# Setup weights in small tiles and a new model of engines and transfers in the planner of a four-layer graph network

## The chip, the cores and the metric

The kernel runs on one core of a Trainium2 chip. The core has five engines with a queue each: TensorE (PE in the profile; its weight loads are shown as PEld), VectorE (DVE), ScalarE (ACT), GpSimd (POOL) and SyncE (SP), which issues most of the transfers. Each engine works through its own queue in order. The metric is the device time of one execution in microseconds (us); lower is better. Before the change it is 3286.79 us, the median of three runs (3286.14 to 3287.27).

## The reference

The input is 64 graphs of 256 nodes with 256 features each (x), and a 256 x 256 integer adjacency of zeros and ones per graph. Four layers follow one another, each on a normalised and rectified copy of x, and each is added to x:

```
h = relu(layernorm(x)); x = x + GAT(h, adj)      # layer 0: 4 heads of 64, slope 0.2, elu
h = relu(layernorm(x)); x = x + typed_GAT(h,adj) # layer 1: 4 heads of 64, slope 0.01,
                                                 #   bias, relu, + h, layernorm per head, gamma, beta
h = relu(layernorm(x)); x = x + GAT(h, adj)      # layer 2: 1 head of 256, slope 0.2
h = relu(layernorm(x))                           # layer 3: three rounds of
for i in range(3):                               #   m = h @ weight[i]
    h = GRU(adj^T @ (h @ weight[i]), h)          #   gates r, z, n from w_ih, w_hh
x = x + h
```

An attention layer projects h to Wh, scores node i against node j with leaky_relu(src_i + dst_j), where src and dst are products of Wh with fixed vectors, masks with the adjacency, takes the softmax over j and sums the rows of Wh with these weights. Everything is fp32.

## The kernel before

**Tiling.** Two graphs make a pair; there are 32 pairs (NP). For a pair, 512 node rows lie as 4 chunks (C) of 128 partitions. The work is written per pair in the functions layer0, layer1, layer2 and gru.

**Setup (group -1).** Weights are loaded once. For each attention layer the score vectors are folded into the weights: score_column multiplies a weight block with a broadcast vector (tensor_mul on VectorE, into a temporary of class g), reduces it, and copies the result into an extra column of w0e, w1e or w2e. There are 12 such products of 128 x 256. The graph convolution's weight[i] and the GRU's w_ih are multiplied once into wc (input_gates, L925), so that a round of the GRU needs adj^T h, then wc, and whh. For that, weight (w3) and w_ih (wih) are loaded into two tiles of class cb4_, one each. The norms of the score columns are checked (check_columns) and the GRU's biases are combined (gate_biases).

**A pair.** norm takes statistics on VectorE (L962, L963), a power on GpSimd (L971, L972) and applies them on ScalarE (L980). transposed turns the result on TensorE (L997). project multiplies with w0e, w1e or w2e (L1019), and ScalarE copies to wh. factors transposes one score column to a row (L1053), takes its exponential (L1060), sends the row to DRAM on ScalarE's queue (rd, L1065) and loads it back from there, broadcast to all partitions, on SyncE's queue into cb (L1066; 1 MB for a layer of 4 heads, class cb4_, of which there are two slots). weights makes the unnormalised attention pt on VectorE from cb and the other factor f (L1087, four instructions a head) and takes the minimum with cap, which holds the mask (L807). attend_head multiplies pt with wh on TensorE (L1107). gru runs three rounds; each has 12 groups of matmuls of 128x512 (gate, L1318: ht with whh, ag with wc), the aggregation with the adjacency (L1304) and transposes (L1332). layer0 also loads x (L1144) and the adjacency (at, L1146, one slot), takes degrees (L1156), casts the adjacency on GpSimd (am) and builds cap (L1164, L1177).

**The order.** Nothing above is issued in the order in which it is written. Each step becomes an operation with an engine, an estimated cost in ns and the buffers it reads and writes. Buffers belong to classes with a fixed number of slots (cb4_: 2, at: 1, g: 9, bank: 8). _Schedule.run first gives each operation a due time, backwards from the end of its pair, (p + 1) x 100000 ns: a successor's due time less 3 times its cost (STRETCH) less HOP. Then it plays the engines forward in a model: whenever an engine is free, it takes the operation with the earliest due time whose inputs are there and whose buffers have a free slot. The sequence that comes out is fixed as the order of each engine's queue on the chip. The model's times exist in this planning alone; on the chip the engines wait for one another through semaphores. In the model, an instruction's result is visible to another engine HOP = 300 ns after its cost, to its own engine at once; a transfer takes its bytes at DMA_RATE plus DMA_LATENCY, and SyncE may issue any number of them ahead.

Vector instructions that go through the helper vec are all shown as L807 in the profile; the tile names tell them apart.

Of the kernel before, what the change touches and what calls it, by code (L numbers as in the profile page):

```python
# [517 lines left out]
SLOPES = (0.2, 0.01, 0.2)  # L518

# [18 lines left out]
class _Schedule:  # L538
# [8 lines left out]
    HOP = 300  # L547
    DMA_LATENCY = 2000
    DMA_RATE = 250.0
    STRETCH = 3.0  # L550

# [67 lines left out]

    def run(self):  # L620
        ops = self.ops
        for o in reversed(ops):
            late = self.end[o.group]
            for s in o.succs:
                if s.group == o.group or o.group not in self.end or o.group < 0:
                    late = min(late, s.due - self.STRETCH * s.cost - self.HOP)
            if o.nbytes:
                late -= self.DMA_LATENCY + o.nbytes / self.DMA_RATE
            o.due = late
# [17 lines left out]
        while True:  # L647
            for e in engines:
                if not idle[e]:
                    continue  # L650
                held = []
                while able[e]:
# [6 lines left out]
                    if all(len(self.free[c]) >= n for c, n in need.items()):  # L659
# [9 lines left out]
                        post(clock + o.cost, "free", o)  # L669
# [7 lines left out]
            while events and events[0][0] == clock:  # L677
                _, _, kind, o = heapq.heappop(events)
                if kind == "free":
                    idle[o.engine] = True  # L680
                    t = clock
                    if o.nbytes:
                        self.dma_free = max(self.dma_free, clock) + o.nbytes / self.DMA_RATE
                        t = self.dma_free + self.DMA_LATENCY
                        post(t, "done", o)
                    else:
                        post(t + self.HOP, "done", o)
                        for s in o.succs:
                            if s.engine == o.engine:
                                s.waits -= 1  # L690
                                if s.waits == 0:
                                    heapq.heappush(able[s.engine], (s.due, s.index))
                elif kind == "done":
                    done += 1
                    for s in o.succs:
                        if o.nbytes or s.engine != o.engine:
                            s.waits -= 1
                            if s.waits == 0:
                                heapq.heappush(able[s.engine], (s.due, s.index))
# [9 lines left out]
def _fast_path(  # L709
# [38 lines left out]
    P = 128  # L748
# [66 lines left out]
    def dma(engine, nbytes, emit, reads=(), writes=(), takes=()):  # L815
        op(engine, 450 if engine == "sp" else 120, emit, reads, writes, takes, nbytes)
# [4 lines left out]
    w3, wih = buf("cb4_", [P, L, DC, D]), buf("cb4_", [P, DC, G])  # L821
# [33 lines left out]
    for i in range(L):  # L855
        dma("sp", 1 << 18, lambda i=i: nc.sync.dma_start(
            w3.tile[:, i], w3t[i].rearrange("(c p) d -> p c d", p=P)), (), [(w3, i)])
    dma("sp", 3 << 18, lambda: nc.sync.dma_start(
        wih.tile, wih_t.rearrange("(c p) g -> p c g", p=P)), (), [wih])
# [4 lines left out]
    def score_column(B_we, w_ap, vec_buf, v_ap, dst, k, dc, s):  # L864
# [3 lines left out]
        vec(nc.vector.tensor_mul, 330, view, w_ap, v_ap,  # L868
            reads=[(B_we, (dc, "w")), vec_buf], writes=[tmp])
        col = lambda: cols.tile[:, dc, k : k + heads]  # L870
        vec(nc.vector.tensor_reduce, 330, col, view, AX.X, OP.add, reads=[tmp], writes=[(cols, (dc, k))])
        vec(nc.vector.tensor_copy, 80, dst, col, reads=[(cols, (dc, k))], writes=[(B_we, (dc, s))])
# [47 lines left out]
    def input_gates(i, dc, g0, g1):  # L920
        ps = bank()

        def mm():
            for ec in range(DC):
                nc.tensor.matmul(  # L925
                    ps.tile[:, : g1 - g0],
                    lhsT=w3.tile[:, i, ec, dc * P : (dc + 1) * P],
                    rhs=wih.tile[:, ec, g0:g1],
# [4 lines left out]
        op("pe", (g1 - g0) * 3.4, mm, [(w3, i), wih], [ps])  # L933
        vec(nc.scalar.copy, 150 + (g1 - g0), wc[:, i, dc, g0:g1], lambda: ps.tile[:, : g1 - g0],
            reads=[ps], writes=[(B_wc, (i, dc, g0))], engine="act")

    for i in range(L):
        for dc in range(DC):
            for g0 in (0, 512):
                input_gates(i, dc, g0, min(g0 + 512, G))  # L940
# [8 lines left out]
    op("dve", 300, gate_biases, [bi, bh], [B_bg])  # L949
# [5 lines left out]
    def norm(xt, cls):  # L955
# [19 lines left out]
        vec(nc.vector.scalar_tensor_tensor, 120, lambda: mv.tile[:, 3, :], lambda: mv.tile[:, 0, :], -1.0,  # L975
# [13 lines left out]
    def transposed(xn, cls):  # L989
        ht = buf(cls, [P, DC, S])  # L990

        def block(dc):
# [8 lines left out]
            op("pe", 470, emit, [xn], [ps], takes=[ht])  # L1001
# [7 lines left out]
    def project(ht, we, B_we, heads, width, shift):  # L1009
# [4 lines left out]
        def rows(c):  # L1014
# [12 lines left out]
            op("pe", 910, emit, [ht, B_we], [ps], takes=[wh])  # L1027
# [440 lines left out]
```

## Time and profile before

| | |
|---|---|
| median of the runs | 3286.79 us |
| profiled execution: time, span | 3288.5 us, 3286.6 us |
| mean granted TensorE clock | 0.989 |
| PE busy in 0 to 100, 100 to 200, 200 to 300 us | 60.0, 59.2, 99.8 us |
| PE busy in 3200 to 3287 us | 74.2 us |
| DVE, ACT, POOL busy over the span | 2368.8, 1453.9, 1103.6 us |
| first GRU matmul (L1318) | 170.8 us |
| granted TensorE clock at 120 to 130 us | 0.50 |

The span runs from the first to the last instruction; the rest of an execution's time lies around it. A line of a group reads: line, engine, operation, output tile <- input tiles, shapes, count, then what the engine waited for in brackets. In the chain of waits and in the waits view, "A <- B" means that A stood idle until B was done. For SyncE the queue itself is shown (SPq): its waits are spent by the queue in front of a transfer, with everything behind it.

### The profile page before, as it was taken

To read this page: it belongs to the slowest core of one execution; us is meant where nothing else is said; L and a number is where in the kernel's file an instruction comes from. 1 tells how busy PE (TensorE), PEld (TensorE's weight loads), DVE (VectorE), ACT (ScalarE), POOL (GpSimd) and SP (SyncE) were. 2 spreads that over 40 slices of the span, in tenths; PEclk is the share of its full clock that TensorE was granted. 3 is DMA by queue.
4 is the path that set the end of the run, shared out by engine and by line. 5 is a ranking of instruction groups with operands and counts; after the bars stand their busy time and mean duration, and the time that the engine had idled before them with its cause. 6 is when DMAs were issued, how large, how long until landed. Compare 5 with 4: busy or idle time off the path is not lost.

```text
span 3286.6 us, 49515 instructions
## 1 busy us (share of the span) xinstructions
PE 3184.5 (97%) x19094; PEld 1890.3 (58%) x19094; DVE 2368.8 (72%) x4977; ACT 1453.9 (44%) x2829; POOL 1103.6 (34%) x1096
## 2 busy tenths in 40 slices
PE   6499999999999999999999999999999999999998
PEld 4355555655565565565555555655565565565554
DVE  6947777777777777777777777777777777776752
ACT  4244444544444444444544444544444444444432
POOL 2423332343432334332424432343432334332330
PEclk8799999999999999999999999999999999999999
DMA  4101110111110111011101110111111111011000
GB/s 137 43 21 39 39 43 30 49 38 41 46 47 32 36 43 49 33 44 41 43 30 56 40 43 30 49 37 41 48 38 41 36 43 49 33 36 36 30 10 14
DMA packets 73012, 134.02 MB, mean 41 GB/s; under 512 B 7872, under 2 KB 59840, under 8 KB 64576
## 3 DMA queue, kind: packets, MB, share of 16 engines
q1 hardware_dynamic: 68688, 129.38, 11.3%
q8 instruction: 153, 2.51, 0.3%
q10 hardware_dynamic: 4080, 1.39, 0.2%
q14 instruction: 91, 0.75, 0.1%
HBM read 113.38 MB, written 17.37 MB: 40 GB/s over the span
## 4 chain that ended last, share of the span: by engine, by line
PE 87%; DVE 4%; POOL 4%; issue 1%; ACT 1%; DVEq 0%; POOLq 0%; ACTq 0%
PE bank L1318 56%; PE bank L1107 11%; PE bank L1019 9%; PE bank L1304 5%; PE bank L997 3%; PE bank L1332 2%; POOL mean L1240 1%; DVE o L807 1%; POOL g L807 1%; DVE g L807 1%; POOL o L807 1%; ACT g L807 0%; PE bank L1177 0%; PE bank L1053 0%; DVE hl L807 0%
## 5 line engine op out<-in xcount | busy, mean ns | idle before, releaser
L1318 PE MATMUL bank<-ag,wc 128*128 128x512 f32 x2304 | 1058.7, 597 | 0.0
L1318 PE MATMUL bank<-ht,whh 128*128 128x512 f32 x2304 | 1052.3, 594 | 0.0
L807 ACT ACTIVATE g<-bank,bg 128x512 f32<-128x512 f32 x576 | 395.3, 686 | 1001.3 <-PE bank L1318 995.5
L1318 PEld LDWEIGHTS bank<-ag,wc 128*128 128x128 f32 x2304 | 425.6, 190 | 493.0 <-issue 481.6
L1318 PEld LDWEIGHTS bank<-ht,whh 128*128 128x128 f32 x2304 | 421.0, 190 | 455.3 <-issue 442.6
L807 DVE SCALAR_TENSOR_TENSOR g<-g,g 128x512 f32<-128x512 f32 x384 | 285.7, 744 | 319.8 <-ACT g L807 316.4
L1087 DVE TENSOR_SCALAR pt<-cb,f 128x256 f32<-128x256 f32 x1152 | 399.5, 421 | 114.6 <-PE bank L1107 100.8
L807 POOL TENSOR_TENSOR g<-ht,g 128x512 f32<-128x512 f32 x192 | 321.0, 1688 | 418.3 <-ACT g L807 418.3
L1107 PE MATMUL bank<-wh,pt 128*64 128x65 f32 x9216 | 405.1, 244 | 48.7 <-DVE pt L807 48.4
L1107 PEld LDWEIGHTS bank<-wh,pt 128*64 128x64 f32 x9216 | 331.7, 140 | 186.3 <-issue 122.4
L807 DVE TENSOR_TENSOR pt<-pt,cap 128x1024 f32<-128x1024 f32 x288 | 373.6, 1327 | 3.3
L807 POOL TENSOR_TENSOR o<-o,bias_b 128x512 f32<-128x512 f32 x64 | 92.8, 1450 | 576.5 <-DVE o L807 363.8
L1304 PE MATMUL bank<-am_r,hl 128*128 128x256 f32 x1536 | 236.1, 301 | 5.8 <-DVE hl L807 5.4
L807 ACT ACTIVATE g<-g,bg 128x512 f32<-128x512 f32 x192 | 133.2, 716 | 228.7 <-DVE g L807 228.7
L980 ACT ACTIVATE xn<-xt,mv 128x256 f32<-128x256 f32 x384 | 205.2, 589 | 65.3 <-DVE mv L807 64.9
L971 POOL TENSOR_SCALAR mv<-mv 128x4 f32<-128x4 f32 x128 | 31.1, 243 | 595.3 <-DVE mv L963 553.2
L1304 PEld LDWEIGHTS bank<-am_r,hl 128*128 128x128 f32 x1536 | 196.8, 190 | 40.9 <-issue 24.6
L962 DVE BATCH_NORM_STATS2 st<-xt 128x6 f32<-128x256 f32 x512 | 208.2, 407 | 12.1 <-DMA xt<-in_x_dram 8.8
L807 ACT COPY ht<-bank 128x512 f32<-128x512 f32 x256 | 139.5, 590 | 120.3 <-PE bank L997 114.3
L807 DVE TENSOR_TENSOR g<-g,bank 128x512 f32<-128x512 f32 x192 | 127.6, 683 | 74.8 <-PE bank L1318 74.8
L807 DVE RECIPROCAL rs<-bank 128x4 f32<-128x4 f32 (+1 forms) x384 | 56.3, 164 | 162.4 <-PE bank L1107 162.2
L1034 ACT COPY wh<-bank 128x264 f32<-128x264 f32 (+1 forms) x256 | 96.2, 376 | 132.2 <-PE bank L1019 130.2
(91 smaller groups left out, 3522.4 us busy)
## 6 DMA issues: line engine op xcount, KB each, us to landing
cb<-rd SPq DMA_DIRECT2D x64, 1024.0 KB
xt<-in_x_dram SPq DMA_DIRECT2D x32, 512.0 KB
at<-in_adj_dram SPq DMA_DIRECT2D x32, 512.0 KB
out_dram<-xt SPq DMA_DIRECT2D x32, 512.0 KB
cb<-rd SPq DMA_DIRECT2D x32, 256.0 KB
rd<-row ACTq DMA_DIRECT2D x64, 8.0 KB
cb<-in_L_gnn_w_ih_dram SPq DMA_DIRECT2D x1, 768.0 KB
cb<-in_L_gnn_weight_dram SPq DMA_DIRECT2D x3, 256.0 KB
```

Of the source, the lines that this page charges most:

```text
L807: op(engine, cost, lambda: fn(*[a() if callable(a) else a for a in args], **kw), reads, writes)
L962: nc.vector.bn_stats(st.tile[:, c, :], xt.tile[:, c, :])
L980: op("act", 610, lambda: nc.scalar.activation(xn.tile[:, c, :], xt.tile[:, c, :], AF.Relu, bias=mv.tile[:, 3, c : c + 1], scale=mv.tile[:, ...
L997: nc.tensor.transpose(ps.tile[:, c * P : (c + 1) * P], xn.tile[:, c, dc * P : (dc + 1) * P], ident)
L1019: nc.tensor.matmul(ps.tile[:, : heads * W], lhsT=ht.tile[:, dc, c * P : (c + 1) * P], rhs=we[:, dc].rearrange("p h w -> p (h w)"), start=( ...
L1034: nc.scalar.copy(wh.tile[:, :, c, :], src)
L1087: nc.vector.tensor_scalar(pt.tile[:, b, jc, :].rearrange("p (i n) -> p i n", n=P), cb.tile[:, h, 2 * b : 2 * b + 2, :], f.tile[:, 1, h, c ...
L1107: nc.tensor.matmul(ps[q * Q : (q + 1) * Q], lhsT=pt.tile[:, b, jc, i0 : i0 + Q], rhs=wh.tile[:, h, 2 * b + jc, :w], start=(jc == 0), stop= ...
L1240: nc.gpsimd.tensor_tensor(var.tile, var.tile, nhalf[:, :R], op=OP.pow)
L1304: nc.tensor.matmul(ps.tile[:, b * N : (b + 1) * N], lhsT=hl.tile[:, k, 2 * b + sc, :], rhs=am.tile[:, 2 * b + sc, :], start=(k == 0 and sc ...
L1318: nc.tensor.matmul(ps.tile, lhsT=w[:, dc, g * P : (g + 1) * P], rhs=v.tile[:, dc, :], start=(first and dc == 0), stop=(last and dc == DC - 1),
L1332: nc.tensor.transpose(ps.tile[:, c * P : (c + 1) * P], ht.tile[:, j, c * P : (c + 1) * P], ident)
```

## The change

The diff has five parts.

1. w3 and wih are no longer two tiles of class cb4_ but six tiles of 128 x 2 x 256 of class g (three each), loaded with six transfers of 256 KB. input_gates runs over three blocks of 256 gate columns in place of blocks of 512 and 256.
2. The 12 products of score_column are issued on GpSimd in place of VectorE.
3. The planner holds SyncE back when more than DMA_AHEAD = 2000 ns of transfers are outstanding in its model. DMA_RATE becomes 220.
4. The planner's model of engines: HOP becomes a value per engine, an OVERLAP per engine frees an engine before its result is there, and a follower on the same engine, TensorE's apart, waits for the result and the hop too. Due times use MARGIN = 200 where they used HOP.
5. Estimated costs of many operations are changed, by a few per cent to some 20 per cent, up or down.

PACE names the 100000 that was written out before. The diff, cut:

```diff
+    OVERLAP = {"pe": 0, "act": 90, "dve": 80, "pool": 0, "sp": 0}
+    HOP = {"pe": 250, "act": 120, "dve": 120, "pool": 150, "sp": 0}
     DMA_LATENCY = 2000
-    DMA_RATE = 250.0
+    DMA_RATE = 220.0
+    DMA_AHEAD = 2000
     STRETCH = 3.0
+    MARGIN = 200.0
...
+    def enable(self, ops, able):
+        for o in ops:
+            o.waits -= 1
+            if o.waits == 0:
+                heapq.heappush(able[o.engine], (o.due, o.index))
...
-                    late = min(late, s.due - self.STRETCH * s.cost - self.HOP)
+                    late = min(late, s.due - self.STRETCH * s.cost - self.MARGIN)
...
+                if e == "sp" and self.dma_free > clock + self.DMA_AHEAD:
+                    continue
...
-                        post(clock + o.cost, "free", o)
+                        post(clock + o.cost - self.OVERLAP[e], "free", o)
...
-                        t = self.dma_free + self.DMA_LATENCY
-                        post(t, "done", o)
+                        post(self.dma_free + self.DMA_LATENCY, "done", o)
+                        post(max(clock, self.dma_free - self.DMA_AHEAD), "dma", o)
                     else:
-                        post(t + self.HOP, "done", o)
-                        for s in o.succs:
-                            if s.engine == o.engine:
...
+                        post(clock + self.OVERLAP[o.engine] + self.HOP[o.engine], "done", o)
+                    if o.engine == "pe":
+                        self.enable([s for s in o.succs if s.engine == "pe"], able)
                 elif kind == "done":
                     done += 1
-                    for s in o.succs:
-                        if o.nbytes or s.engine != o.engine:
...
+                    self.enable([s for s in o.succs if s.engine != "pe" or o.engine != "pe"], able)
...
-    w3, wih = buf("cb4_", [P, L, DC, D]), buf("cb4_", [P, DC, G])
+    w3, wih = ([buf("g", [P, DC, D]) for _ in range(3)] for _ in range(2))
...
-    dma("sp", 3 << 18, lambda: nc.sync.dma_start(
-        wih.tile, wih_t.rearrange("(c p) g -> p c g", p=P)), (), [wih])
+    for k in range(3):
+        dma("sp", 1 << 18, lambda k=k: nc.sync.dma_start(
+            wih[k].tile, wih_t.rearrange("(c p) g -> p c g", p=P)[:, :, k * D : (k + 1) * D]), (), [wih[k]])
...
-        vec(nc.vector.tensor_mul, 330, view, w_ap, v_ap,
-            reads=[(B_we, (dc, "w")), vec_buf], writes=[tmp])
+        vec(nc.gpsimd.tensor_tensor, 700, view, w_ap, v_ap, op=OP.mult,
+            reads=[(B_we, (dc, "w")), vec_buf], writes=[tmp], engine="pool")
...
-        op("pe", (g1 - g0) * 3.4, mm, [(w3, i), wih], [ps])
+        op("pe", 870, mm, [w3[i], wih[k]], [ps])
...
-            op("pe", 470, emit, [xn], [ps], takes=[ht])
+            op("pe", 445, emit, [xn], [ps], takes=[ht])
...
-            op("pe", 910, emit, [ht, B_we], [ps], takes=[wh])
+            op("pe", 895, emit, [ht, B_we], [ps], takes=[wh])
...
-        op("pe", 150, emit_t, [wh], [ps])
+        op("pe", 115, emit_t, [wh], [ps])
...
-                op("dve", 440, lambda b=b, jc=jc: emit(b, jc), [cb, f], [(pt, (b, jc))])
+                op("dve", 425, lambda b=b, jc=jc: emit(b, jc), [cb, f], [(pt, (b, jc))])
...
-        op("pe", 980, emit, [pt, wh], [ps], takes=[o])
+        op("pe", 1040, emit, [pt, wh], [ps], takes=[o])
...
-            op("pe", 250, emit, parts(cap_n, (2 * b, 2 * b + 1)), [(ps, b)], takes=[cap])
+            op("pe", 230, emit, parts(cap_n, (2 * b, 2 * b + 1)), [(ps, b)], takes=[cap])
...
-            op("pe", 880, lambda: attend(ps.tile[:, : D + 1], pt, wh, c, 0, D + 1), [pt, wh], [ps])
+            op("pe", 910, lambda: attend(ps.tile[:, : D + 1], pt, wh, c, 0, D + 1), [pt, wh], [ps])
...
-            op("pe", 920, emit, [hl, am], [ps], takes=[ag])
+            op("pe", 1060, emit, [hl, am], [ps], takes=[ag])
...
-            op("pe", 1740, emit, [v, B_w], [ps])
+            op("pe", 1725, emit, [v, B_w], [ps])
...
-                vec(nc.gpsimd.tensor_tensor, 1330, lambda: d.tile, lambda: ht.tile[:, j, :],
+                vec(nc.gpsimd.tensor_tensor, 1500, lambda: d.tile, lambda: ht.tile[:, j, :],
```

The other changed costs are of the same kind.

## The prediction

> **What bounds the kernel now.** I read the page's busy table and slices first, then the busy time by stretch of the first 175 us, then the waits of SyncE's DMA queue, then the timeline around the stretch where TensorE is idle.
>
> ```profile
> PE 3184.5 (97%) x19094; PEld 1890.3 (58%) x19094; DVE 2368.8 (72%) x4977; ACT 1453.9 (44%) x2829; POOL 1103.6 (34%) x1096
> PE   6499999999999999999999999999999999999998
> DVE  6947777777777777777777777777777777776752
> ```
>
> TensorE is the bound for all but the first two slices (82 us each) and the end. The rest, 3286.6 - 3184.5 = 102 us, is what can be won without doing less matmul work. The chain of waits shows how regular the middle is: the same piece comes back every three pairs.
>
> ```profile
> 1672.34 15.45 PE bank L1318 x36
> 1968.31 15.45 PE bank L1318 x36
> ```
>
> (1968.31 - 1672.34)/3 = 98.66 us per pair, which I call the period. In the middle TensorE waits for almost nothing; this is the waits view for 300 to 3100 us (total, times, longest, in us):
>
> ```profile
> PE bank L1304 <- DVE hl L807: 5.4, 9, 0.6
> PE bank L1332 <- DVE ht L807: 0.7, 1, 0.7
> ```
>
> So 6 us in 2800 is all that a better order can take from waits there. The start is different. Busy time by stretch (window, its length, then each engine):
>
> ```profile
> 0.00:16.60 16.60, 0.03 (x1) 0.03 (x1) 7.74 (x27) 3.73 (x6) 4.12 (x13) 1.00 0.68 197
> 16.60:30.00 13.40, 12.81 (x48) 8.75 (x49) 10.11 (x45) 8.15 (x19) 3.96 (x7) 1.00 0.85 277
> 30.00:49.80 19.80, 19.80 (x101) 15.14 (x100) 3.46 (x9) 14.91 (x33) 6.37 (x13) 1.00 0.28 97
> 49.80:110.00 60.20, 33.86 (x535) 29.01 (x533) 54.95 (x128) 15.61 (x37) 10.09 (x10) 0.77 0.20 75
> 110.00:167.00 57.00, 20.07 (x228) 15.81 (x228) 51.19 (x111) 12.66 (x26) 33.30 (x30) 0.68 0.07 24
> ```
>
> Columns after the length are PE, PEld, DVE, ACT, POOL. From 49.8 to 167 us VectorE is busy 106.1 of 117.2 us and TensorE only 53.9: there VectorE is the bound, because the GRU of pair 0, which feeds TensorE, can't start until pair 0 has passed three attention layers. From 30 to 49.8 us VectorE works 3.46 us and is idle 16.3. The timeline names why:
>
> ```profile
> 26.74 0.34 ACTq L1065 DMA_DIRECT2D rd<-row  x1
> 45.31 0.82 SPq L1066 DMA_DIRECT2D cb<-rd  x2
> 49.81 3.97 DVE L1087 TENSOR_SCALAR pt<-cb,f 128x256 f32<-128x256 f32 x12 [2.14 <-DMA cb<-rd]
> 170.84 2.42 PE L1318 MATMUL bank<-ht,whh 128*128 128x512 f32 x4
> ```
>
> The row goes out at 26.74, the broadcast load that brings it back is issued at 45.31, the first attention weights follow at 49.81, the first GRU matmul at 170.84. The queue's own waits say what it stood behind:
>
> ```profile
> SPq L1146 <- DVE rs L1156: 11.3, 1, 11.3
> SPq L1066 <- PE bank L925: 10.0, 1, 10.0
> SPq L1146 <- ACT cap_n L1150: 3.5, 1, 3.5
> ```
>
> First a load of the adjacency of pair 2 (L1146) waits for its one slot till 35.2; then the cb load waits 10.0 us for the input-gate products (L925), since w3 and wih sit in both cb4_ slots. Later, where nothing is in its way, the same step takes:
>
> ```profile
> 224.72 0.25 ACTq L1065 DMA_DIRECT2D rd<-row  x1
> 225.88 0.34 SPq L1066 DMA_DIRECT2D cb<-rd  x1
> 229.97 1.38 DVE L1087 TENSOR_SCALAR pt<-cb,f 128x256 f32<-128x256 f32 x4 [1.23 <-DMA cb<-rd]
> ```
>
> That is 1.2 us and 4.1 us, 5.3 in all, against 23.1 at the start.
>
> **What the Trainium skill says.** "DMA: Bandwidth & Descriptors", section on the anatomy of one DMA: a semaphore wait of a DMA is spent on the issuing sequencer before dispatch. The trace agrees: the two SP waits above hold everything queued after them. "SBUF — State Buffer", section "Who interferes with whom": VectorE and GpSimd share a port pair under an exclusive lock, also when a tensor_tensor reads two SBUF inputs. It fits: at 118.65 a GpSimd product of 128x512 takes 3.18 us and at 123.13 one takes 1.26, with VectorE active beside the first. "GPSIMD Engine Reference", section 3.1, prices tensor_tensor at 1.96 times VectorE.
>
> **The change part by part.** (1) Small tiles for w3 and wih: both cb4_ slots are free from the start, so the 10.0 us wait goes. (2) The other stall, pair 2's adjacency load ahead of it, goes only if the planner puts the cb load ahead in SP's order. The limit on outstanding transfers is in the planner alone and adds no wait on the chip; it only changes the order in SP's queue. With it, SP in the model holds back and picks by due time when there is room. In the model the row is back near 21 us: adding costs and hops from the load of x, through norm, transpose and projection. By then the model's rate of 220 bytes/ns allows 4.5 MB; what is more urgent (x and adjacency of pairs 0 and 1, w0, w1, vectors, w2) is 3.9 MB, and 2.25 MB of w3, wih and whh, which the present order already puts ahead of x of pair 2, are still mostly out. So I take the cb load to come before pair 2's adjacency. Then it is issued at 26.74 + 1.2 to 1.4 = 28.1 and lands with 4.1 to 4.5 (the same step at 45.31 took 4.5): VectorE starts at 32.2 to 32.6 in place of 49.81, a shift of 17.2 us. If the DMA queue is not drained by then (277 GB/s in 16.6 to 30), it is up to 1 MB / 277 GB/s = 4 us later.
>
> From there the stage is VectorE's, so the shift carries through to the first GRU matmul, less what is now free: the 3.46 us that VectorE does in 30 to 49.8 (degrees, checks) then fall into the busy stage. 17.2 - 3.5 = 13.7 us; if the 11.1 us of VectorE idle time in 49.8 to 167 take them up, 17.2. I take 15. TensorE has as much work before the GRU as now, so what the GRU's start gains the end gains. The input gates are the same work, cut into 18 groups in place of 12; now they run during the wait (TensorE is busy 32.6 of the 33.2 us from 16.6 to 49.8), afterwards they lie in TensorE's 63 idle us of 49.8 to 167, and cost nothing, unless a late weight in TensorE's order holds an attention head: bounds 0 to 5, taken 0. The loads are now 6 of 256 KB in place of 4: two more issues at 0.45 us on SP, ahead of or behind a waiting cb load, 0 to 1 us.
>
> (3) Setup products on GpSimd: 12 of 128x256. VectorE has 0.42 us each, 5 us in all, which lie before 22.9 us, where it is not the bound; GpSimd would need 0.63 (half of 1.26) to 0.82 (0.42 x 1.96), so 8 to 10 us, and is busy 14.5 of the first 49.8. In front of it queue the norm's power and the cast of the adjacency. The projection of pair 0 starts at 19.9, the w0 columns are ready at 12.7 now; 4 products are then 1 to 2 us later and still early. Taken as 0, bounds -1 to +3. (4) Nine of the g slots less six until the gates are done: before that only temporaries and four elu tiles want them. 0 to 2 us, taken 0.
>
> (5) The model of overlap, hop and costs (also: a follower on the same engine, TensorE's apart, now waits for the hop) changes the order of every pair; it adds no instruction and no wait by itself. Adding its new TensorE costs for a pair gives 98.2 us against 98.66 measured, and the seen waits are 0.2 us per pair, so the gain is at most 0.46 x 30 = 14 us and likelier the 6 of waits. The loss has no such bound. The new delays are still on the safe side of what the trace shows: a ScalarE gate at 3183.42 is followed by VectorE at 3184.14, 0.72 us, where the new model says 700 + 120 and the old 700 + 300; a gate matmul group at 3181.50 by ScalarE at 3183.42, 1.92 us, against 1725 + 250. I take -2, bounds -10 to +45.
>
> Sum: -15 - 2 = -17. The profiled execution took 3288.5 us with a span of 3286.6 (1.9 us around it), so it would take 3271.5; from the median of the timed runs, 3286.8, I forecast 3270.
>
> **The rivals.** The forecast: 3262 to 3280, chance 0.55.
>
> A larger gain, 0.13: the order brings pair 0 through its layers ahead of pairs 1 and 2, and half of the 63 idle us of TensorE go, about -32: 3255. For it: the idle stretches are long (20.9 us before 127.93). Against it: STRETCH stays at 3 and the group ends stay 100 us apart, which is what mixes the pairs.
>
> No change, 0.13: the early cb load only lets VectorE do more of pairs 1 and 2, or sits behind another wait in SP's queue (adjacency of pair 1 or 2), and pair 0's GRU starts within 5 us of where it does now: 3285. The 11.3 us SP wait speaks for it; it is the way in which the change wouldn't do what it says.
>
> Slower, 0.19: the order in the middle. The new model frees VectorE 80 ns and ScalarE 90 ns earlier per instruction; with 4977/32 = 155 VectorE instructions a pair it believes in 12 us more room than the old one. But locks stretch them (the minimum of pt with cap has a mean of 1327 ns in the page's groups, and is planned at 1240), and TensorE in its fixed order then waits behind an attention head or a split. It decides from 15/30 = 0.5 us per pair; at 1 us per pair the time is 3286.8 - 15 + 30 = 3302. For it: TensorE is at 99 to 100% in the middle, so there is far more to lose than to win. Against it: VectorE is at 74%, and the delays are measured safe.
>
> **The numbers.** A measurement of this kernel tells 0.2%, 6.6 us, from no change. Faster than 3280: 0.53 of the forecast, 0.13 and 0.04 of the others, 0.70. Within: 0.12 (mostly the no-change case). Slower than 3293: 0.18 (0.16 of the slower case, 0.02 of the no-change case with a late weight on top). The range 3250 to 3298 leaves out half of the larger gain and about half of the slower case.
>
> **What would show it.** Right: the wait of L1066 for L925 is gone, the first L1087 starts near 33 us, the first GRU matmul near 155, and the period stays 98.4 to 98.7 us. Wrong at step 2: an adjacency load still stands before the first cb load. Wrong at step 5: a period above 99.2, with new TensorE waits for VectorE in 300 to 3100 us. If VectorE starts early but the GRU doesn't, the shift was spent on other pairs.

## The result, and the profile after

The kernel after takes 3344.18 us (median of four runs, 3343.88 to 3345.76), the kernel before 3287.03 (3286.14 to 3287.68) beside it: a ratio of 1.0175, 95% interval 1.0157 to 1.0193. It is 57 us slower where 17 us less were forecast, and it lies outside the range of 3250 to 3298. The profiled execution took 3345.8 us with a span of 3344.0 and a mean granted TensorE clock of 0.988 (0.989 before).

The busy table and two rows of slices of the page after:

```profile
PE 3205.0 (96%) x19118; PEld 1895.1 (57%) x19118; DVE 2360.1 (71%) x4965; ACT 1447.0 (43%) x2835; POOL 1177.2 (35%) x1108
PE   6499999999999999999999999999999999999998
DVE  6837767767677677777777677677777777676652
```

The slices look as before: nothing stands out anywhere. TensorE's idle time grew from 102 us to 3344.0 - 3205.0 = 139. That is 37 us of the loss. The other 20 us are a longer busy time of TensorE (3205.0 against 3184.5) for the same products but for the cut of the input gates; the page's ends of matmuls are modelled, so a short wait may be hidden in it. VectorE is busy 9 us less, GpSimd 74 us more. Where the time grew is read from the transfers that store a finished pair. Timeline after (start, duration, engine, instruction; SPq is SyncE's queue):

```profile
28.02 0.42 SPq L1073 DMA_DIRECT2D cb<-rd  x1
...
31.62 0.45 SPq L1153 DMA_DIRECT2D at<-in_adj_dram  x1
...
33.55 3.96 DVE L1094 TENSOR_SCALAR pt<-cb,f 128x256 f32<-128x256 f32 x12 [3.03 <-DMA cb<-rd]
...
170.65 2.59 PE L1325 MATMUL bank<-ht,whh 128*128 128x512 f32 x4
...
262.29 0.39 SPq L1399 DMA_DIRECT2D out_dram<-xt  x1
...
3263.66 0.39 SPq L1399 DMA_DIRECT2D out_dram<-xt  x1
```

The same two stores before (the second line takes in that of pair 31):

```profile
267.18 0.38 SPq L1392 DMA_DIRECT2D out_dram<-xt  x1
...
3206.52 75.05 SPq L1392 DMA_DIRECT2D out_dram<-xt  x2
```

Pair 0 is stored at 262.29 (before: 267.18, so 4.9 us earlier), pair 30 at 3263.66 (before: 3206.52). The 30 pairs between take 3001.4 us in place of 2939.3: +62.0. After the last of these stores 80.3 us are left (before 80.1). So -4.9 + 62.0 + 0.2 = 57.3, which is the difference of the spans: all of the loss is in the middle. The chain of waits after, by engine and two of its steps:

```profile
PE 83%; DVE 11%; POOL 3%; ACT 2%; issue 1%; DMA 0%; ACTq 0%; DVEq 0%; POOLq 0%
...
1096.36 10.32 PE bank L1325 x24
...
1297.27 10.32 PE bank L1325 x24
```

The pattern now repeats every two pairs, not three, and takes 200.91 us: 100.45 a pair, where before had 98.73 as a mean over pairs 3 to 27. VectorE has 11% of the chain (before 4%). TensorE's waits in 300 to 3100 us (total, times, longest) are 49.0 us together, before 6.4:

```profile
PE bank L1026 <- DVE hl L813: 16.7, 25, 0.7
PE bank L1339 <- DVE ht L813: 16.6, 29, 1.1
PE bank L1114 <- ACT ht L813: 13.9, 15, 0.9
PE bank L1114 <- DVE o L813: 1.1, 1, 1.1
PE bank L1311 <- DVE hl L813: 0.7, 1, 0.7
```

L1026 is the projection, L1339 the transposes, L1114 the attention heads, L813 the helper vec (L1019, L1332, L1107 and L807 before). These are many waits of 0.6 to 0.9 us on average, up to one a pair at each place, which no slice shows. The second part of the result is the start; busy time by stretch (window, its length, PE, PEld, DVE, ACT, POOL):

```profile
30.00:49.80 19.80, 19.80 (x173) 17.16 (x171) 11.80 (x31) 9.41 (x24) 4.01 (x2) 0.95 0.51 181
49.80:110.00 60.20, 37.94 (x426) 31.12 (x424) 52.12 (x122) 22.45 (x54) 21.93 (x25) 0.78 0.20 71
110.00:167.00 57.00, 27.12 (x294) 21.78 (x295) 50.15 (x103) 11.05 (x23) 24.96 (x26) 0.65 0.05 15
```

The first cb load went out at 28.02 and ahead of the adjacency, as foretold (28.1), and VectorE started at 33.55 (foretold 32.2 to 32.6). It works 11.80 us in 30 to 49.8 where it worked 3.46. But the first GRU matmul stands at 170.65, as before (170.84). Of the 8.3 us done early, 2.6 only make up for less work before 30 us (15.2 against 17.9), 1.9 are more work done by 167 us, and 3.9 come back as idle time later (102.3 busy of 117.2 us from 49.8 to 167, before 106.1). One thing that stops VectorE early is TensorE's order: the first attention heads stand behind 8.8 us of input gates (L932), and VectorE then waits for the heads.

```profile
35.78 8.80 PE L932 MATMUL bank<-g,g 128*128 128x256 f32 x40
...
44.51 3.02 PE L1114 MATMUL bank<-wh,pt 128*64 128x65 f32 x96
...
45.71 1.38 DVE L1094 TENSOR_SCALAR pt<-cb,f 128x256 f32<-128x256 f32 x4 [4.80 <-PE bank L1114]
```

### The profile page after: what moved, and what is told of

The parts are those of the page before. It is cut to its first block, busy times and chain, and to the rows that moved or that the text cites. A ratio compares the mean times of both kernels' runs of the same rounds, so it can differ in the third digit from the quotient of the medians.

```text
span 3344.0 us, 49644 instructions
## 1 busy us (share of the span) xinstructions
PE 3205.0 (96%) x19118; PEld 1895.1 (57%) x19118; DVE 2360.1 (71%) x4965; ACT 1447.0 (43%) x2835; POOL 1177.2 (35%) x1108
## 4 chain that ended last, share of the span: by engine, by line
PE 83%; DVE 11%; POOL 3%; ACT 2%; issue 1%; DMA 0%; ACTq 0%; DVEq 0%; POOLq 0%
PE bank L1325 54%; PE bank L1114 11%; PE bank L1026 8%; PE bank L1311 5%; DVE g L813 3%; PE bank L1004 2%; POOL g L813 2%; DVE pt L1094 2%; PE bank L1339 2%; DVE ht L813 1%; ACT g L813 1%; DVE xt L1258 1%; DVE o L813 1%; DVE hl L813 1%; PE bank L932 0%
## 5 line engine op out<-in xcount | busy, mean ns | idle before, releaser
L813 ACT ACTIVATE g<-bank,bg 128x512 f32<-128x512 f32 x576 | 393.9, 687 | 1006.6 <-PE bank L1325 907.6
L813 DVE SCALAR_TENSOR_TENSOR g<-g,g 128x512 f32<-128x512 f32 x384 | 312.4, 816 | 483.4 <-ACT g L813 463.9
L813 POOL TENSOR_TENSOR g<-ht,g 128x512 f32<-128x512 f32 x192 | 343.0, 1799 | 434.6 <-ACT g L813 434.6
L1114 PE MATMUL bank<-wh,pt 128*64 128x65 f32 x9216 | 406.2, 245 | 59.0 <-DVE pt L813 37.6
L1114 PEld LDWEIGHTS bank<-wh,pt 128*64 128x64 f32 x9216 | 332.6, 140 | 187.8 <-issue 100.9
L1094 DVE TENSOR_SCALAR pt<-cb,f 128x256 f32<-128x256 f32 x1152 | 407.7, 423 | 29.2 <-DMA cb<-rd 20.7
L813 DVE TENSOR_TENSOR pt<-pt,cap 128x1024 f32<-128x1024 f32 x288 | 342.1, 1215 | 1.0
L813 POOL TENSOR_TENSOR o<-o,bias_b 128x512 f32<-128x512 f32 x64 | 106.1, 1657 | 574.2 <-DVE o L813 508.6
L813 ACT ACTIVATE g<-g,bg 128x512 f32<-128x512 f32 x192 | 135.3, 719 | 218.6 <-DVE g L813 217.7
L813 DVE TENSOR_TENSOR g<-g,bank 128x512 f32<-128x512 f32 x192 | 128.7, 683 | 133.6 <-PE bank L1325 133.6
L1311 PEld LDWEIGHTS bank<-am_r,hl 128*128 128x128 f32 x1536 | 197.0, 190 | 21.8 <-issue 16.5
L813 ACT COPY ag<-bank 128x512 f32<-128x512 f32 x192 | 112.7, 587 | 138.9 <-PE bank L1311 138.8
L1041 ACT COPY wh<-bank 128x264 f32<-128x264 f32 (+1 forms) x256 | 94.5, 376 | 158.0 <-PE bank L1026 157.4
L1026 PE MATMUL bank<-w0e,ht 128*128 128x264 f32 x512 | 137.9, 407 | 19.7 <-DVE hl L813 18.3
```

Of the source, the lines that this page charges most:

```text
L813: op(engine, cost, lambda: fn(*[a() if callable(a) else a for a in args], **kw), reads, writes)
L1026: nc.tensor.matmul(ps.tile[:, : heads * W], lhsT=ht.tile[:, dc, c * P : (c + 1) * P], rhs=we[:, dc].rearrange("p h w -> p (h w)"), start=( ...
L1041: nc.scalar.copy(wh.tile[:, :, c, :], src)
L1094: nc.vector.tensor_scalar(pt.tile[:, b, jc, :].rearrange("p (i n) -> p i n", n=P), cb.tile[:, h, 2 * b : 2 * b + 2, :], f.tile[:, 1, h, c ...
L1114: nc.tensor.matmul(ps[q * Q : (q + 1) * Q], lhsT=pt.tile[:, b, jc, i0 : i0 + Q], rhs=wh.tile[:, h, 2 * b + jc, :w], start=(jc == 0), stop= ...
L1311: nc.tensor.matmul(ps.tile[:, b * N : (b + 1) * N], lhsT=hl.tile[:, k, 2 * b + sc, :], rhs=am.tile[:, 2 * b + sc, :], start=(k == 0 and sc ...
```

## The experiments

The expectations name their theories by letters, as they were held before each run. What the runs share is in one table; waits are TensorE's in 300 to 3100 us, the period is the mean distance of the stores of pairs 3 to 27, the gate is the first GRU matmul. The code cuts show the lines that matter of each edit.

| run | median us | ratio to before [95%] | period | waits | gate |
|---|---|---|---|---|---|
| after | 3344.18 | 1.0175 [1.0157, 1.0193] | 100.45 | 49.0 | 170.7 |
| e1_tiles_only | 3278.79 | 0.9976 [0.9967, 0.9985] | 98.68 | 5.7 | 161.1 |
| e2_old_engine_model | 3304.13 | 1.0052 [1.0035, 1.0068] | 99.66 | 20.0 | 160.2 |
| e3_hop300 | 3304.98 | 1.0057 [1.0040, 1.0074] | 99.21 | 35.5 | 168.6 |
| e4_bank_fifo | 3308.97 | 1.0069 [1.0052, 1.0086] | 99.24 | 26.1 | 169.1 |
| e5_tiles_pool | 3278.02 | 0.9976 [0.9966, 0.9985] | 98.64 | 5.8 | 162.6 |
| e6_tiles_dma_model | 3304.40 | 1.0055 [1.0038, 1.0072] | 99.74 | 19.7 | 158.0 |
| e7_old_follower | 3337.40 | 1.0155 [1.0138, 1.0172] | 100.76 | 51.8 | 160.7 |
| e8_overlap0 | 3285.35 | 0.9997 [0.9989, 1.0006] | 98.55 | 0.5 | 170.4 |
| e9_overlap_act_only | 3280.66 | 0.9983 [0.9976, 0.9990] | 98.65 | 3.0 | 153.0 |
| e10_limit_only | 3282.08 | 0.9987 [0.9980, 0.9994] | 98.63 | 6.6 | 164.9 |
| e11_overlap0_old_dma | 3301.96 | 1.0047 [1.0034, 1.0061] | 99.32 | 21.9 | 167.0 |
| e12_tiles_pool_fifo | 3277.75 | 0.9975 [0.9964, 0.9985] | 98.58 | 5.8 | 162.1 |
| e13_before_dve_overlap | 3333.11 | 1.0142 [1.0127, 1.0158] | 100.02 | 25.3 | 174.9 |
| e14_overlap_dve40 | 3268.64 | 0.9944 [0.9929, 0.9959] | 98.08 | 5.1 | 165.1 |
| e15_dve0_fifo | 3270.80 | 0.9953 [0.9939, 0.9966] | 98.35 | 1.2 | 153.3 |
| e16_no_lock | 3264.25 | 0.9931 [0.9916, 0.9946] | 98.07 | 0.3 | 159.7 |
| e17_no_lock_dve0 | 3258.85 | 0.9919 [0.9904, 0.9934] | 98.13 | 0.0 | 148.3 |
| e18_dve40_fifo | 3264.30 | 0.9934 [0.9920, 0.9947] | 98.00 | 4.1 | 163.2 |

**The setup alone, and all but the engine model.** e1 is the kernel before with part 1; e2 is the kernel after with parts 4 and 5 undone.

```diff
-    w3, wih = buf("cb4_", [P, L, DC, D]), buf("cb4_", [P, DC, G])      (e1, on before)
+    w3, wih = ([buf("g", [P, DC, D]) for _ in range(3)] for _ in range(2))
```

```diff
-    HOP = {"pe": 250, "act": 120, "dve": 120, "pool": 150, "sp": 0}    (e2, on after)
+    HOP = 300
-                        post(clock + o.cost - self.OVERLAP[e], "free", o)
+                        post(clock + o.cost, "free", o)
```

> The kernel before with the six small setup tiles alone; old engine model, old costs, products on VectorE, no limit on transfers. Theory M (the loss of 57 us is the new engine model in the middle): the period stays 98.7 us per pair and the time is 3270 to 3288. Theory S (the setup itself disturbs what follows): 3300 or more. For the start: if the early cb load is worth what the prediction said, 3270; if the start gives it back, 3284 to 3290.

> The changed kernel with parts 4 and 5 undone: the old HOP of 300, no overlap, the old rule for followers, the old margin and costs; small tiles, products on GpSimd and the limit on transfers stay. Theory M: the period is back at 98.7 us and the time is 3270 to 3290. Theory S: it stays at 3330 to 3345.

The tiles alone bring 8 us, at an unchanged period, and the gate 9.7 us earlier. With the engine's old model, the middle still loses about a microsecond a pair: so parts 2 and 3 together were not innocent, which neither theory had foreseen. Parts 4 and 5 together cost the remaining 40 us. No run changes the costs of part 5 alone; some of them move by more than the 20 per cent named above (a transfer issued on ScalarE from 120 to 320 ns, a small VectorE step from 120 to 160).

**Parts 2 and 3.** e5 is e1 with the products on GpSimd, e10 is e5 with the limit on outstanding transfers, e6 is e1 with the limit and the rate of 220.

```diff
-        vec(nc.vector.tensor_mul, 330, view, w_ap, v_ap,               (e5)
+        vec(nc.gpsimd.tensor_tensor, 700, view, w_ap, v_ap, op=OP.mult,
+                if e == "sp" and self.dma_free > clock + self.DMA_AHEAD:   (e10, e6)
+                    continue
-    DMA_RATE = 250.0                                                   (e6)
+    DMA_RATE = 220.0
```

> Small tiles and products on GpSimd, old engine model, no limit on transfers (e1 plus part 2). The run with both part 2 and part 3 took 3304 us at a period of 99.66 us, e1 took 3279 at 98.68. If the products on GpSimd leave another state behind from which the plan locks into a worse cycle: a period near 99.7 and 3300 or more. If the transfer model does it: 98.7 and 3275 to 3285.

> Small tiles, products on VectorE, old engine model, but the rate of 220 and the limit on outstanding transfers (e1 plus part 3). The mirror image of e5: if the transfer model shifts the order in every pair, a period near 99.7 and 3295 to 3305; if the products do it, 98.7 and 3270 to 3285.

> Small tiles, products on GpSimd, old engine model, rate 250, and the limit on outstanding transfers alone (e5 plus half of part 3). e5 took 3278 at a period of 98.64; with rate and limit it was 3304 at 99.66. If the limit reorders SyncE's queue in the middle and with it the rest: 99.7 and 3300 to 3306. If the rate of 220 does it, which makes every cb load later in the model and its due time earlier: 98.6 and 3276 to 3281.

The products cost nothing, the limit alone 4 us (one of its 20 executions took 15358 us, which nothing here explains; without it the median is 3281.95). e6 costs 25 us more than e1. The rate alone is the difference of e2 and e10, which differ in nothing else: 22 us. It enters the planner's due times and the times at which transfers land, and so changes the order of the middle. The waits of e6 (12.9 us of the aggregation for hl, 6.2 of L1182 for wh) explain about half of its loss; the rest is not seen as a wait, but as a longer busy time of TensorE, 99.0 us a pair against 98.5 in e1 (busy in 300 to 3100 us, times the period over 2800).

**Numbers of the engine model, one at a time, on the kernel after.**

```diff
+    HOP = {"pe": 300, "act": 300, "dve": 300, "pool": 300, "sp": 300}  (e3)
+                    if not o.nbytes:                                   (e7)
+                        self.enable([s for s in o.succs if s.engine == o.engine], able)
+    OVERLAP = {"pe": 0, "act": 0, "dve": 0, "pool": 0, "sp": 0}        (e8)
+    OVERLAP = {"pe": 0, "act": 90, "dve": 0, "pool": 0, "sp": 0}       (e9)
```

> The changed kernel with HOP 300 for every engine in place of 250, 120, 120, 150, 0; all else as changed. If the short hops make TensorE's order too tight (slots handed on before the chip has freed them), the TensorE waits of 49 us in 300 to 3100 us fall to under 15 and the time to about 3290 to 3300. If the overlap or the costs are the cause: 3335 to 3345.

> The changed kernel with the old rule for followers on the same engine: they may follow as soon as the engine is free. If the new rule, which sends other work ahead of a dependent VectorE step, is what makes gates and splits late: the period falls from 100.45 towards 99.2 or below, 3300 to 3310. If it is of no account: 3335 to 3345.

> The changed kernel with no overlap: VectorE and ScalarE are taken for their full cost, 12 us more VectorE time per pair in the model. The fourth case of the prediction said that this overlap makes the plan too tight. If so, the period falls to 99.2 or below and the time to 3300 to 3310; if the short hops alone do it (the run with HOP 300 won 39 us), it stays at 3330 to 3345.

> The changed kernel with the overlap of VectorE at 0 and ScalarE's left at 90. With both at 0 the period was 98.55 us and the time 3285. If VectorE's overlap is the cause (the plan counts on a VectorE that the shared port with GpSimd makes late), the period is again 98.5 to 98.9 and the time 3283 to 3295. If ScalarE's overlap is: it stays near 3340. If any perturbation may fall into another cycle: something in between, with no rule.

The follower's rule is worth 7 us, and not in the middle, where the period of e7 is even longer. VectorE's overlap of 80 ns is worth 63.5 us (e9), more than the whole loss; ScalarE's of 90 is rather a gain (e8 less e9, 4.7 us). A longer hop also takes 39 us back, with waits that fall to 35.5 us only, where under 15 were expected; that it gives room in another place is my reading. With e9 the start comes true too, as its timeline shows:

```profile
152.99 3.78 PE L1325 MATMUL bank<-ht,whh 128*128 128x512 f32 x4 [0.32 <-ACT ht L813]
...
254.65 0.39 SPq L1399 DMA_DIRECT2D out_dram<-xt  x1
```

**Is the DMA model a second cause?** e11 is e8 with the old rate and no limit.

```diff
+    DMA_RATE = 250.0
+    DMA_AHEAD = 1e9
```

> The changed kernel with no overlap, rate 250 and no limit: hops, followers, margin and costs stay as changed. If the transfer model costs 25 us in any setting: 3260. If it only tips the plan from one cycle into another, which the period of 98.55 with it and without overlap says, nothing is left to win in the middle (TensorE's own work is near 98.4 us a pair) and only the start can differ: 3275 to 3290.

Here the old transfer model is 17 us slower, which neither expectation had, while in e6 the new one was 25 us slower than the old. So the number has no sign of its own. As I read it, the plan settles with either in one repeating cycle or in another, and some of these wait on the chip; what picks the cycle isn't shown.

**The banks.** The planner gives out the lowest-numbered free PSUM bank; e4 (on after) and e12 (on e5) give out the one that has been free longest.

```diff
-                                b.slot = heapq.heappop(self.free[b.cls])
+                                free = self.free[b.cls]
+                                b.slot = free.pop(0) if b.cls == "bank" else heapq.heappop(free)
```

> The changed kernel with the eight PSUM banks handed out longest-free first in place of lowest number first; the order in the model is the same, only which bank. If TensorE waits because a bank that the model has just freed is taken again at once (waits of L1026 for the hl copy and of L1114 for the ht copy, 31 us in 300 to 3100), these go and the time falls by about 31 us, to 3313. If the waits are for data (L1339 for ht, 17 us) or come from the order alone, it stays at 3340 to 3345.

> Small tiles, products on GpSimd, old engine model, and the banks longest-free first. The bank order took 35 us of waits from the changed kernel, but e5 has only some 6 us of TensorE waits in 300 to 3100 us, so at most that: 3272 to 3278. It would be the fastest of all versions. If the bank order takes nothing here: 3276 to 3280.

In after the projection takes the bank that VectorE's hl is just reading, and stands until it is read. "Perfetto Trace Analysis" of the Trainium skill, section on matmuls, asks that independent groups rotate through the banks so that evacuation overlaps. In e4 it agrees, 35 us; in e12 there is nothing to gain (0.3 us). TensorE's waits in e4, same view as above: the waits of the projection are gone, those of the transposes remain.

```profile
PE bank L1343 <- DVE ht L817: 14.6, 30, 1.0
PE bank L1118 <- DVE pt L817: 10.6, 16, 0.7
```

**The overlap alone, and half of it.** e13 is the kernel before with VectorE's overlap and nothing else; e14 is after with 40 in place of 80.

```diff
+    OVERLAP = {"pe": 0, "act": 0, "dve": 80, "pool": 0, "sp": 0}       (e13, on before)
+    OVERLAP = {"pe": 0, "act": 90, "dve": 40, "pool": 0, "sp": 0}      (e14, on after)
```

> The kernel before, with one thing of the change alone: the plan takes VectorE as free 80 ns before the end that it used to assume, and its results as ready 80 ns later (OVERLAP of VectorE 80, all hop delays 300 as before). Theory V (a VectorE that the plan believes freer than it is leaves no slack for stretched instructions): slower than before by 15 us or more, period 99.2 or longer, TensorE waits for VectorE in 300 to 3100 of 20 us or more (before: 6). Rival T (the overlap does harm only together with the other new numbers, which tip the plan from one repeating cycle to another): within 8 us of before, period 98.6 to 98.9.

> The kernel after with VectorE's overlap halved to 40 ns. Theory V: the loss follows the size, so the time lies between that with 0 (3280.7) and with 80 (3344.2), about 3295 to 3330, period 99.1 to 100.1. Rival T (tipping between cycles): at or near one of the two ends, under 3288 or over 3338.

e13 shows it: one number, 46.6 us slower (3333.1 against 3286.5), with one wait a pair for the GRU's state:

```profile
PE bank L1333 <- DVE ht L808: 25.0, 28, 1.9
PE bank L1108 <- DVE pt L808: 0.3, 1, 0.3
```

e14 refuted the expectation of a loss in proportion: half the overlap is the best of the three sizes (0: 3280.7, 40: 3268.6, 80: 3344.2). It beats both kernels. Its time lies where rival T had put it (under 3288), while e13 had refuted rival T: a number of the model can cost by itself, and can also move the plan in ways that its size doesn't tell. In the middle e14's gain over e9 isn't in the waits (5.1 us against 3.0) but in TensorE's busy time a pair, 97.9 us against 98.5; why it differs isn't shown.

**Why VectorE is late.** e16 keeps the order, costs and buffers of after, and takes GpSimd's long two-input instructions away, so that it leaves out that part of the computation; e17 is the same with VectorE's overlap 0. For d, likewise for bias, gamma and beta:

```diff
-                vec(nc.gpsimd.tensor_tensor, 1500, lambda: d.tile, lambda: ht.tile[:, j, :], ...
+                def fill():
+                    nc.gpsimd.tensor_tensor(d.tile[:, :1], ht.tile[:, j, :1], n.tile[:, :1], op=OP.subtract)
+                    for _ in range(2):
+                        nc.gpsimd.memset(d.tile[:, 1:], 0.0)
+                op("pool", 1500, fill, [(ht, j), n], [d])
```

> The kernel after with the same order, costs and buffers, but without the long two-input instructions on GpSimd: the difference of old state and candidate in the GRU, and bias, gamma and beta of the first layer, each replaced by an addition over one or two elements, which keeps the waits, and two fills of the same tile, so that this part of the computation is left out. Theory L (VectorE and GpSimd stretch one another by their shared lock, and the plan has no room for the stretch): TensorE's waits for VectorE in 300 to 3100 fall from 49 to under 15 us, the SCALAR_TENSOR_TENSOR g from g,g goes from 816 ns to about 700, period 98.5 to 99.2, time down by 40 us or more. Rival P (the plan itself is at fault, stretch or not: VectorE's queue holds instructions in an order that is late even when each takes its planned time): 3330 to 3345, waits over 40 us.

> The kernel of e16, so without GpSimd's long two-input instructions (that part of the computation is left out), and with VectorE's overlap 0. It is the control of e16: with those instructions in place the overlap is worth 63.5 us (3344.2 against 3280.7). Theory L (the overlap hurts only because the lock stretches what the plan has no room for): without them it is worth nothing, 3255 to 3273, within 9 us of e16's 3264.3, waits of TensorE under 3 us. Rival P (the long instructions on GpSimd cost about 80 us in any order, and the overlap costs 63 beside that): 3190 to 3210.

GpSimd stays nearly as busy (1111.9 us against 1177.2; for d, 685 + 2 x 523 ns on average in place of 1851), so little can come from GpSimd being done earlier. Yet the loss is gone, and with it nearly all that the overlap is worth: 80 or 0 now differ by 5.4 us, not 63.5. GpSimd's instructions cost something in either order, but 79.9 us with the overlap of 80 (after less e16) and 21.8 with 0 (e9 less e17). One place shows how. Timeline of after:

```profile
1188.54 1.48 POOL L813 TENSOR_TENSOR o<-o,beta_b 128x512 f32<-128x512 f32 x1
...
1188.88 1.68 DVE L813 SCALAR_TENSOR_TENSOR g<-g,g 128x512 f32<-128x512 f32 x1
...
1190.49 0.68 DVE L813 TENSOR_TENSOR o<-o,mean 128x512 f32<-128x512 f32 x1
...
1191.09 0.68 DVE L813 SCALAR_TENSOR_TENSOR ht<-g,g 128x512 f32<-128x512 f32 x1
1191.25 1.66 POOL L813 TENSOR_TENSOR o<-o,gamma_b 128x512 f32<-128x512 f32 x1 [1.23 <-DVE o L813]
...
1191.69 1.75 DVE L1258 TENSOR_TENSOR xt<-xt,o 128x512 f32<-128x512 f32 x1
...
1191.92 0.63 PE L1339 MATMUL bank<-ident,ht 128*128 128x128 f32 x4 [0.47 <-DVE ht L813]
1192.38 1.06 PE L1026 MATMUL bank<-w0e,ht 128*128 128x264 f32 x4
...
1193.37 1.27 DVE L813 TENSOR_TENSOR hl<-bank,hl 128x512 fp32r<-128x512 f32 x2
...
1194.11 1.16 PE L1026 MATMUL bank<-w0e,ht 128*128 128x264 f32 x4 [0.67 <-DVE hl L813]
```

The same place of the same order in e16:

```profile
1154.91 1.11 POOL L1237 MEMSET o<- 128x512 f32 x2
...
1155.83 0.69 DVE L813 SCALAR_TENSOR_TENSOR g<-g,g 128x512 f32<-128x512 f32 x1 [0.20 <-ACT g L813]
...
1156.44 0.68 DVE L813 TENSOR_TENSOR o<-o,mean 128x512 f32<-128x512 f32 x1
...
1157.04 0.68 DVE L813 SCALAR_TENSOR_TENSOR ht<-g,g 128x512 f32<-128x512 f32 x1
...
1157.64 0.69 DVE L1263 TENSOR_TENSOR xt<-xt,o 128x512 f32<-128x512 f32 x1
...
1158.25 0.68 DVE L813 TENSOR_TENSOR hl<-bank,hl 128x512 fp32r<-128x512 f32 x1
1158.39 0.60 PE L1344 MATMUL bank<-ident,ht 128*128 128x128 f32 x4
...
1158.82 1.95 PE L1026 MATMUL bank<-w0e,ht 128*128 128x264 f32 x8
```

In e16 five VectorE instructions follow one another every 0.60 us, and TensorE waits for none of them. In after the first takes 1.68 and the fourth 1.75 us, each beside a two-input GpSimd instruction; TensorE waits 0.47 us for ht, which stands behind the first, and 0.67 us for hl, which stands behind the fourth. The projection's eight matmuls are x8 in one line in e16 and two lines of x4 in after; from the first VectorE instruction to their end it is 6.39 us in place of 4.94. The pace of 0.60 us against a duration of 0.68 also says that the overlap of 80 ns is measured right where nothing stretches an instruction. Groups, mean in ns after the busy time, after and then e16, in 300 to 3100 us:

```profile
L813 DVE SCALAR_TENSOR_TENSOR g<-g,g 128x512 f32<-128x512 f32 x336 | 275.5, 823 | 365.7 <-ACT g L813 348.1 <-POOL g L813 17.5
```

```profile
L813 DVE SCALAR_TENSOR_TENSOR g<-g,g 128x512 f32<-128x512 f32 x342 | 235.9, 690 | 405.1 <-ACT g L813 381.0 <-POOL g L1388 22.4 <-ACT ht L813 0.7
```

"SBUF — State Buffer", section "Who interferes with whom", says that a VectorE instruction with two SBUF inputs contends with a GpSimd instruction that reads SBUF, and not with one that only writes it. The fills only write, and the stretch is gone: the trace agrees. The stretch is not new, though: in e9, which is 63.5 us faster than after, the same group has 877 ns. What after lacks is room for it.

```profile
L813 DVE SCALAR_TENSOR_TENSOR g<-g,g 128x512 f32<-128x512 f32 x340 | 296.8, 877 | 348.1 <-ACT g L813 321.3 <-POOL g L813 26.7
```

**Both repairs.** e15 and e18 have the bank rule of e4, with VectorE's overlap 0 and 40.

> The kernel after with VectorE's overlap 0 and the PSUM banks given out longest-free first, the two repairs together. Theory V: the overlap's removal has left few waits (3.0 us in 300 to 3100), so the banks can give 3 us at most: 3275 to 3281, period 98.5 to 98.65. Rival B (the lowest-numbered bank is the root and the overlap only brings it out): the same sum, so no number here tells V from B; but over 3290 would show that the two are not independent repairs and that a third thing tips the order.

> The kernel after with VectorE's overlap 40 and the PSUM banks given out longest-free first. e14 has 4.2 us of waits for VectorE in the transposes and 0.9 us beside, so if the two repairs are independent the banks give 0 to 5 us here: 3263 to 3269, period 98.0 to 98.1. If the plan tips between repeating cycles whatever the numbers mean, it is as likely to be 3280 or more.

The bank rule adds 9.9 us to e9, more than its waits allowed, and 4.3 us to e14. e18 is the fastest kernel here that computes everything: 0.66% below before and 2.4% below after (3264.3 of 3344.2).

## Why the prediction was wrong

Step 1 was right: no cb load waits for the input gates.

Step 2 was right on the queue and in the start of VectorE to a microsecond, but not for its reason. The limit isn't needed for it: with the tiles alone (e1) the first cb load also went out at 28.02 and VectorE started at 32.62; with the limit (e10) the load went out at 31.05. In e1:

```profile
28.02 0.34 SPq L1067 DMA_DIRECT2D cb<-rd  x1
31.15 0.37 SPq L1147 DMA_DIRECT2D at<-in_adj_dram  x1
...
32.62 4.86 DVE L1088 TENSOR_SCALAR pt<-cb,f 128x256 f32<-128x256 f32 x12 [2.00 <-DMA cb<-rd]
```

Wrong was "the shift carries through to the first GRU matmul". With nearly the same start of VectorE the gate came 9.7 us earlier in e1, 0.4 in e8, 17.9 in e9 and 0.2 in after. So the order decides, and not the start alone. Two things that hold the gate in after can be named. The input gates hold the attention heads, for which the prediction had bounds of 0 to 5 and took 0: VectorE's wait is 4.8 us. And GpSimd's long instructions: in the same order without them (e16) the gate stood at 159.7 us, 11.0 earlier. Nor does the end gain what the gate gains: in e9 17.9 us at the gate are 12.5 at the store of pair 0 and 8.4 at the end of the span. Why isn't shown.

Step 3 was right: e5 equals e1, and the products took 0.68 to 0.69 us each on GpSimd (foretold 0.63 to 0.82). Step 4 has no run of its own. In after SyncE's queue waits 6.7 and 4.0 us before the loads of w3 and wih for VectorE's steps on w2e (L862 and L865), as I read it for the slots of class g that these hold; the cb load goes out 2.9 us after its row, where 1.2 to 1.4 were foretold, so the cost is about 1.5 us, within the bounds. The rate was not in the sum at all: it was taken for a matter of the start, and e2 less e10 shows 22 us in the middle.

Step 5 failed, and with it the sign. It was taken as -2 and measured +40 (after less e2), inside its bounds of -10 to +45. In the order in which the runs build on one another the parts come to -7.6 us for the tiles, -0.8 for the products, +3.9 for the limit, +22.2 for the rate and +40.1 for parts 4 and 5; e11 shows that these sizes hold in this order only.

"I take -2" rested on the sentence "The new delays are still on the safe side of what the trace shows". That is true of delays between two engines and was measured at places where nothing was stretched. It isn't what decides: an engine's queue is a sum of durations, and one part of the plan's reserve against the stretches by GpSimd was that it counted 80 ns too much for each VectorE operation. The code makes 137 VectorE operations a pair (not 155, which are instructions), so 11.0 us a pair went out of the reserve at once. The stretch could be seen in the trace of before. At 123.13 the prediction read a GpSimd product of 1.26 us as one without VectorE beside it, but this stands there:

```profile
123.20 1.73 DVE L1251 TENSOR_TENSOR xt<-xt,o 128x512 f32<-128x512 f32 x1 [2.49 <-POOL o L807]
```

Here VectorE is the one that is stretched. From four groups of after the stretch can be summed, with e16's 690 ns as the measure: (823 - 690) x 336 for g, (1218 - 690) x 56 for o from mean and o, (1218 - 690) x 54 for xt from xt and o, and (957 - 690) x 56 ns for o from o and mean are 118 us, 4.2 us for each of the 28 pairs in 300 to 3100 us. An overlap of 40 leaves 5.5 us, an overlap of 80 nothing. That these two sizes explain why 40 is good and 80 is not is argued from the sums, not shown. The rival "slower: the order in the middle" named this mechanism, the lock included, and was priced at 1 us a pair with a chance of 0.19; it was 1.72 a pair. Its counter-argument, "VectorE is at 74%", failed since a mean share says nothing of 0.5 us at one place of each pair.

Still open: about half of the loss in e2, e6 and e13 isn't seen as a wait of TensorE but as a longer busy time for the same matmuls, and which cycle the plan falls into (e6 against e11) could not be foreseen from a number. That GpSimd's instructions are also behind the loss of e13 was not tried.

## What to carry to other kernels

Where an order is fixed by a planner, a duration that is right for an undisturbed instruction can be a worse number than one that is too long: what is cut from the model is cut from the reserve, and the bound engine can pay for it in waits of about a microsecond or less each. Cut in steps (here 0, 40, 80 ns gave 3281, 3269, 3344 us), and judge by the period: the bound engine's total waits show a part of it only (e14 has more of them than e9 and is faster). Before trusting a plan, look for instructions in the trace that take much longer than planned (here 1.68 and 1.75 us, where 0.70 was planned), and ask what stands behind each in its queue.

## What the runs showed of the hardware

Two-input VectorE instructions of 128x512 took 0.68 to 0.69 us in e16 and, in the place shown, 1.68 and 1.75 us in after beside a two-input GpSimd instruction; fills on GpSimd over the same tiles and for about the same time left them at 0.69. Such an instruction followed another after 0.60 us, 80 ns before its end. How much these stretches cost depended on the order: without the GpSimd instructions the order of after gained 79.9 us and that of e9 21.8, and with them e14 ran at 98.08 us a pair, as fast as the order of after without them (98.07).
